# A four-layer graph network on one core: layer 2's aggregation by single graphs, with an earlier form of the setup

## The chip, the cores and the metric

The kernel runs on one core of a Trainium2 chip. The time is the device time of one execution in microseconds, the median of several runs. The engines are named as in the profile: PE (TensorE, matmuls), PEld (its weight loads), DVE (VectorE), ACT (ScalarE), POOL (GpSimd) and SP (which issues most of the DMA transfers).

## What is computed

There are 128 graphs of 64 nodes with 256 features each, and one adjacency matrix for all. Four layers follow each other, each as `x = layernorm(x + layer(x))`.

```python
# layer 0: attention over the adjacency matrix
Wh = h @ W;  e = leaky_relu(Wh@a1[:, None] + Wh@a2[None, :]);  e = where(adj == 0, -inf, e)
h_prime = softmax(e) @ Wh
# layer 1: attention over a list of 512 edges (src, dst), 4 heads
Xq, Xv = H @ W_lin.T, H @ W_val.T
e = (leaky_relu(Xq[:, src] + Xq[:, dst]) * a).sum(-1) + log(adj[src, dst] + eps)
Y = segment_sum(segment_softmax(e, src) * Xv[:, dst], src) @ W_out.T
# layer 2: normalised aggregation and two batch-normed products
A_norm = adj + eye;  dinv = rsqrt(deg);  A_hat = A_norm * dinv[:, None] * dinv[None, :]
agg = einsum('nm,bmd->bnd', A_hat, x)
out = batchnorm(relu(batchnorm(agg @ W1.T + b1)) @ W2.T + b2)
# layer 3: two graph products, then LSTMs over windows of 1 to 4 nodes
```

The change concerns the line `agg`, and the work done once at the start: weights and indices are loaded, the edges are sorted by source, and matrices are built that gather by matmul.

## The kernel before

A block `q` is 8 graphs, 512 tokens, as 4 chunks of 128 tokens (two graphs each); there are 16 blocks. Layers 0, 1 and the first product of layer 2 are interleaved in one main loop: while block `q` goes through the edges of layer 1 (`l1_graph`), block `q+2` goes through layer 0, and block `q-3` through the end of layer 1 and the aggregation.

```python
# the aggregation, L402 to L408: aht is A_hat twice, on the diagonal of a 128x128 matrix
def v_c(q):
    x2 = L1.pop(q)["x2"]
    for k in range(KD):
        p_ = bank([PQ, P])
        for c in range(PQ):
            nc.tensor.matmul(p_[:, c, :], x2[:, c, k * P:(k + 1) * P], aht, start=True, stop=True)
        nc.scalar.activation(A[:, q, k * QT:(k + 1) * QT], p_.rearrange("p c t -> p (c t)"), AF.Copy)
```

The product of attention and values in layer 1 (L381) already goes by single graphs, in tiles of 64 rows and 64 columns:

```python
for c in range(PQ):
    for h in range(HEADS):
        for s in range(2):
            r = slice(s * N, (s + 1) * N)
            r0 = (h % 2) * 64
            nc.tensor.matmul(pY[s][r0:r0 + 64, h // 2, c, :], v[r, c, h * 64:(h + 1) * 64],
                             am[r, c * HEADS + h, :], start=True, stop=True)
```

The setup. Its scratch tiles lie in A, the big array that holds the blocks' results later (`su.tile`):

```python
load_x(0)
nc.scalar.dma_start(w0[:, :, :D], i["L0_gnn_W"]...)
nc.scalar.dma_start(aL0, i["L0_gnn_a"].partition_broadcast(P))
nc.sync.dma_start(row_i, i["L1_gnn_src"].partition_broadcast(P))
# ... the columns of indices, the adjacency matrix, load_x(1)
nc.scalar.dma_start(wq[:, :, :D], i["W_linT"]...)
# ... aL1, acol, wv

def own(q, shape, name):     # block 0 of layer 0 has its tiles in A, the others in the pool
    return work.tile(shape, F32, name=name, bufs=1) if q else su.tile(shape, F32, name)

perm = [work.tile([P, E], F32R, name="hi", bufs=4) for c in range(EC)]

def setup_l0():              # L415, L416: two more columns for w0
    ...
        nc.vector.tensor_mul(tmp, w0[:, :, :D], aL0[:, None, n * D:(n + 1) * D].to_broadcast([P, KD, D]))
        nc.vector.reduce_sum(w0[:, :, D + n], tmp, axis=AX.X)

def setup_ends():            # L466: the sorted edges by matmul with the permutation
    for n in range(2):
        pe_ = bank([E])
        for c in range(EC):
            nc.tensor.matmul(pe_, wide[n][:, c, :], perm[c], start=c == 0, stop=c == EC - 1)
        nc.vector.tensor_copy(ends[:, n, :], pe_)
    # ... and 16 matmuls of two columns (L471)

l0_a(0); setup_l0(); ...; l0_b(0); setup_order(); l0_c(0); l0_a(1); setup_ends()
l0_b(1); l0_d(0); setup_gather(); setup_queries(); l0_e(0); l0_c(1); setup_signs()
l0_d(1); l1_t(0); l1_qv(0, 0); l0_e(1); l1_qv(0, 1)
# (each on a line of its own in the kernel)
wout = weights(wa, "wout", i["W_outT"]); w1 = ...; w2 = ...
setup = [setup_zero, setup_segments, setup_bias, setup_pairs]
setup += [lambda c=c: setup_count(c) for c in range(EC)]
setup += [setup_place, setup_adjacency]      # one of these after each step of the main loop
```

The main loop, and in it the edge products and their split in two parts (L316, L319, L320):

```python
nc.tensor.matmul(z, L1[q]["qs"][c][:, s, k * P:(k + 1) * P], gath_r, start=True, stop=True)
nc.scalar.activation(hi, z, AF.Relu)
nc.vector.scalar_tensor_tensor(lo, z, 0.0, hi.bitcast(F32), op0=OP.max, op1=OP.subtract)
```

Of the kernel before, what the change touches and what calls it, by code (L numbers as in the profile page):

```python
# [40 lines left out]
def kernel(ctx: ExitStack, tc: tile.TileContext, i, out):  # L41
# [59 lines left out]
    nc.vector.memset(bd, 0.0)  # L101
    bdT = const.tile([P, P], F32, name="bdT")
# [8 lines left out]
    with ExitStack() as two:  # L111
# [17 lines left out]
        class su:  # L129

            free = NQ * 2 * QT

            @classmethod
            def tile(cls, shape, dtype, name):
                size = 1
                for n in shape[1:]:
                    size *= n
                cls.free -= size
                t = A.rearrange("p q c -> p (q c)")[:shape[0], cls.free:cls.free + size]
                t = t if dtype == F32 else t.bitcast(dtype)  # L140
                if len(shape) == 3:
                    t = t.rearrange("p (a b) -> p a b", b=shape[2])
                elif len(shape) == 4:
                    t = t.rearrange("p (a b c) -> p a b c", b=shape[2], c=shape[3])
                return t


        load_x(0)
        w0 = wa.tile([P, KD, D + 2], F32, name="w0")
        nc.scalar.dma_start(w0[:, :, :D], i["L0_gnn_W"].rearrange("(k p) c -> p k c", p=P))  # L150
        aL0 = su.tile([P, 2 * D], F32, name="aL0")
        nc.scalar.dma_start(aL0, i["L0_gnn_a"].partition_broadcast(P))
        col_i = su.tile([P, EC, 2], I32, name="col_i")
        row_i = su.tile([P, E], I32, name="row_i")
        nc.sync.dma_start(row_i, i["L1_gnn_src"].partition_broadcast(P))
        for n, e in enumerate(("L1_gnn_src", "L1_gnn_dst")):
            nc.sync.dma_start(col_i[:, :, n], i[e].rearrange("(c p) -> p c", p=P))
        for s in range(2):
            nc.sync.dma_start(bd[s * N:(s + 1) * N, s * N:(s + 1) * N], i["adj"])
# [5 lines left out]
        aL1 = su.tile([P, D], F32, name="aL1")  # L165
        nc.scalar.dma_start(aL1, i["L1_gnn_a"].rearrange("h d -> (h d)").partition_broadcast(P))
        acol = su.tile([P, KD], F32, name="acol")
        nc.sync.dma_start(acol, i["L1_gnn_a"].rearrange("h d -> (h d)").rearrange("(c p) -> p c", p=P))
        nc.sync.dma_start(wv, i["W_valT"].rearrange("(k p) c -> p k c", p=P))
# [16 lines left out]
        def own(q, shape, name):  # L186

            return work.tile(shape, F32, name=name, bufs=1) if q else su.tile(shape, F32, name)

        def transposed(src, q=1):  # L190

            t = own(q, [P, KD, QT], "tT")
            for k in range(KD):
                p_ = bank([PQ, P])
                for c in range(PQ):
                    nc.tensor.transpose(p_[:, c, :], src[:, c, k * P:(k + 1) * P], ident)  # L196
                nc.scalar.activation(t[:, k, :], p_.rearrange("p c t -> p (c t)"), AF.Copy)
            return t
# [8 lines left out]
        def l0_a(q):  # L207
            L0[q] = {"x": xin.pop(q)}
            L0[q]["xT"] = transposed(L0[q]["x"], q)

        def l0_b(q):
            xT = L0[q]["xT"]
            wh = L0[q]["wh"] = own(q, [P, PQ, D + 2], "wh")
# [7 lines left out]
            sb = L0[q]["sb"] = own(q, [P, PQ, P], "sb")  # L221
            nc.gpsimd.tensor_copy(sb, wh[:, :, D + 1:].to_broadcast([P, PQ, P]))

        def l0_c(q):
# [4 lines left out]
            t = own(q, [P, PQ, P], "lr")  # L229
# [14 lines left out]
        def l0_d(q):  # L244
            e = L0[q]["e"]
            p_ = bank([PQ, P])
            for c in range(PQ):
                nc.tensor.transpose(p_[:, c, :], e[:, c, :], ident)
            eT = L0[q]["eT"] = own(q, [P, PQ, P], "eT")
            nc.scalar.activation(eT, p_, AF.Copy)  # L250
# [151 lines left out]
        def v_c(q):  # L402
            x2 = L1.pop(q)["x2"]
            for k in range(KD):
                p_ = bank([PQ, P])
                for c in range(PQ):
                    nc.tensor.matmul(p_[:, c, :], x2[:, c, k * P:(k + 1) * P], aht, start=True, stop=True)  # L407
                nc.scalar.activation(A[:, q, k * QT:(k + 1) * QT], p_.rearrange("p c t -> p (c t)"), AF.Copy)  # L408


        def setup_l0():

            tmp = su.tile([P, KD, D], F32, name="tmp")
            for n in range(2):
                nc.vector.tensor_mul(tmp, w0[:, :, :D], aL0[:, None, n * D:(n + 1) * D].to_broadcast([P, KD, D]))  # L415
                nc.vector.reduce_sum(w0[:, :, D + n], tmp, axis=AX.X)  # L416


        iota_e = su.tile([P, E], F32, name="iota_e")
# [6 lines left out]
        for s in range(2):  # L426
            nc.gpsimd.iota(node[s * N:(s + 1) * N, :], pattern=[[0, 1]], base=0, channel_multiplier=1,
                           allow_small_or_imprecise_dtypes=True)
        for n in range(2):
            nc.gpsimd.memset(spads[n], 0.0)  # L430
        ends = su.tile([P, 2, E], F32, name="ends")
        cols = su.tile([P, EC, 2], F32, name="cols")
        ohT = su.tile([P, 2, E], F32, name="ohT")
        ones = su.tile([P, P], F32, name="ones")
        nc.gpsimd.memset(ones, 1.0)
        eps8 = su.tile([P, 1], F32, name="eps8")
        nc.gpsimd.memset(eps8, 1e-8)
        again = su.free

        perm = [work.tile([P, E], F32R, name="hi", bufs=4) for c in range(EC)]  # L440
        wide = [work.tile([P, EC, P], F32R, name="lo", bufs=4) for n in range(2)]
        col_r = work.tile([P, EC, 2], F32R, name="lo", bufs=4)

        def setup_order():
            col_f = su.tile([P, EC, 2], F32, name="col_f")
            nc.vector.tensor_copy(col_f, col_i)
            nc.vector.tensor_copy(col_r, col_f)
            key_r = su.tile([P, E], F32, name="key_r")
            key_c = su.tile([P, EC], F32, name="key_c")
            nc.vector.tensor_copy(key_r, row_i)  # L450
            nc.vector.scalar_tensor_tensor(key_r, key_r, float(E), iota_e, op0=OP.mult, op1=OP.add)
            nc.vector.scalar_tensor_tensor(key_c, col_f[:, :, 0], float(E), iota_c, op0=OP.mult, op1=OP.add)
            for n in range(2):
                nc.gpsimd.tensor_copy(wide[n], col_f[:, :, n:n + 1].to_broadcast([P, EC, P]))
            rank = su.tile([P, EC], F32, name="rank")
            less = su.tile([P, E], F32, name="less")
            for c in range(EC):
                nc.vector.tensor_scalar(less, key_r, key_c[:, c:c + 1], 0.0, op0=OP.is_lt, op1=OP.add,
                                        accum_out=rank[:, c:c + 1])
                nc.vector.tensor_scalar(perm[c], iota_e, rank[:, c:c + 1], None, op0=OP.is_equal)  # L460

        def setup_ends():
            for n in range(2):
                pe_ = bank([E])
                for c in range(EC):
                    nc.tensor.matmul(pe_, wide[n][:, c, :], perm[c], start=c == 0, stop=c == EC - 1)  # L466
                nc.vector.tensor_copy(ends[:, n, :], pe_)
            pcol = bank([EC, 2])
            for r in range(EC):
                for c in range(EC):  # L470
                    nc.tensor.matmul(pcol[:, r, :], perm[c][:, r * P:(r + 1) * P], col_r[:, c, :],  # L471
                                     start=c == 0, stop=c == EC - 1)
            nc.vector.tensor_copy(cols, pcol)

        def setup_gather():

            nc.vector.tensor_scalar(ohT, ends, node, None, op0=OP.is_equal)
            nc.vector.tensor_add(gath_r, ohT[:, 0, :], ohT[:, 1, :])

        def setup_queries():  # L480

            tmp = su.tile([P, KD, D], F32, name="tmp2")
            nc.vector.tensor_mul(tmp, wq[:, :, :D], aL1[:, None, :].to_broadcast([P, KD, D]))
            for k in range(KD):
                nc.vector.reduce_sum(wq[:, k, D:], tmp[:, k, :].rearrange("p (h d) -> p h d", h=HEADS), axis=AX.X)
            nc.vector.scalar_tensor_tensor(aL1, aL1, -1.0, aL1, op0=OP.mult, op1=OP.max)
            nc.vector.tensor_scalar_mul(aL1, aL1, 1.0 - SLOPE)
            nc.vector.tensor_mul(wq[:, :, :D], wq[:, :, :D], aL1[:, None, :].to_broadcast([P, KD, D]))

        def setup_signs():  # L490
            below = su.tile([P, KD], F32, name="below")
            nc.vector.tensor_scalar(below, acol, 0.0, None, op0=OP.is_lt)
            nc.vector.scalar_tensor_tensor(acol, acol, 0.0, below, op0=OP.is_gt, op1=OP.subtract)
# [20 lines left out]
        l0_d(1)  # L514
        l1_t(0)
        l1_qv(0, 0)
        l0_e(1)
        l1_qv(0, 1)


# [465 lines left out]
```

## Time and profile before

| what | us |
|---|---|
| time, median of 3 (2338.16 to 2341.32) | 2340.56 |
| span of the profiled execution | 2338.7 |
| PE busy | 2227.4 |
| DVE busy | 1016.9 |
| ACT busy | 911.3 |
| aggregation, L407, 256 instructions, PE busy | 34.2 |
| edge products, L316, 256 instructions, PE busy | 110.6 |
| LSTM products, L873 and L879, PE busy | 801.4 and 435.9 |

A row of a group names line, engine and operation, then output and inputs, the shape, the number of instructions, the busy time and the mean of one in ns, and last the idle time before them with what ended it. A row of the timeline has the start and duration in us, then the same. In the chain, start and duration stand before the engine and line. A row with several instructions covers the time from the first's start to the last's end. The main loop runs until about 700 us; from there the rest of layer 2 and layer 3 follow, which the change does not touch.

### The profile page before, as it was taken

The numbers are of one execution on the slowest core, as the hardware profiler recorded it, in microseconds if no ns is written. First come the engines' busy times: TensorE is split into PE (matmuls) and PEld (weight loads), VectorE is DVE, ScalarE is ACT, GpSimd is POOL, SyncE is SP. The second block draws the span as 40 slices with busy tenths as digits, with TensorE's granted clock in tenths as the row PEclk, the third lists the DMA queues.
The fourth block names the chain that finished last, engine by engine and source line by source line (L and its number), as shares of the span: only waits on it lengthen the run. The fifth ranks groups of instructions, "written<-read, shape, count | busy, mean of one in ns | idle before, by whom it ended". The sixth has DMA issues, their size and how long they took to land.

```text
span 2338.7 us, 25909 instructions
## 1 busy us (share of the span) xinstructions
PE 2227.4 (95%) x9649; PEld 1536.6 (66%) x9649; DVE 1016.9 (43%) x2317; ACT 911.3 (39%) x1885; POOL 412.5 (18%) x536
## 2 busy tenths in 40 slices
PE   6989999999999997999999999999999999999996
PEld 5767777777654445577578578568568568568475
DVE  7666776777744444232332332332332422422322
ACT  3755565556434701333233233233333333333331
POOL 2123233233220002011211211110210210210101
PEclk8999999999999998999999999999999999999998
DMA  3022023202224002000100100100100100100100
GB/s 116 19 39 48 29 47 57 39 30 37 39 39 108 18 0 96 3 19 8 47 19 1 54 19 1 55 19 1 54 19 1 54 19 1 46 9 1 36 0 28
DMA packets 126654, 74.50 MB, mean 32 GB/s; under 512 B 81856, under 2 KB 117312, under 8 KB 126272
## 3 DMA queue, kind: packets, MB, share of 16 engines
q1 hardware_dynamic: 124672, 70.87, 12.3%
q8 instruction: 76, 1.25, 0.2%
q0 software_dynamic: 1024, 1.05, 0.2%
q10 hardware_dynamic: 832, 0.92, 0.1%
q14 instruction: 50, 0.41, 0.1%
HBM read 44.25 MB, written 28.57 MB: 31 GB/s over the span
## 4 chain that ended last, share of the span: by engine, by line
PE 87%; DVE 6%; ACT 3%; POOL 1%; DMA 1%; issue 1%; SPq 0%; POOLq 0%; DVEq 0%; ACTq 0%
PE l L873 32%; PE l L879 18%; PE g L827 5%; PE pz L735 5%; PE pz L671 5%; PE e L307 3%; PE g L835 2%; PE m L282 2%; PE m L217 2%; PE m L395 2%; PE z L316 2%; PE m L285 2%; PE m L407 1%; PE m L196 1%; PE m L381 1%
## 5 line engine op out<-in xcount | busy, mean ns | idle before, releaser
L873 PE MATMUL l<-H,wih 128*128 128x256 f32 (+2 forms) x2496 | 801.4, 472 | 0.4 <-DVE H L844 0.2
L873 PEld LDWEIGHTS l<-H,wih 128*128 128x128 f32 x2496 | 467.2, 191 | 246.5 <-issue 158.8
L879 PE MATMUL l<-hid,whh 128*128 128x256 f32 (+2 forms) x1536 | 435.9, 437 | 0.0
L879 PEld LDWEIGHTS l<-hid,whh 128*128 128x128 f32 x1536 | 291.8, 190 | 128.4 <-issue 61.2
L885 ACT ACTIVATE gate_i<-l,bias 128x256 f32<-128x256 f32 (+2 forms) x176 | 100.3, 570 | 646.1 <-PE l L879 514.7
L888 DVE TENSOR_TENSOR gate_i<-gate_i,gate_g 128x256 f32<-128x256 f32 (+2 forms) x96 | 47.8, 498 | 571.2 <-ACT gate_g L885 571.2
L889 POOL TENSOR_TENSOR cell<-gate_f,cell 128x256 f32<-128x256 f32 (+2 forms) x96 | 83.7, 872 | 1018.5 <-ACT gate_f L885 1018.5
L320 DVE SCALAR_TENSOR_TENSOR lo<-z,hi 128x512 fp32r<-128x512 f32 x256 | 167.5, 680 | 61.5 <-ACT hi L319 60.2
L319 ACT ACTIVATE hi<-z 128x512 fp32r<-128x512 f32 x256 | 143.9, 597 | 105.6 <-PE z L316 104.4
L82 POOL TENSOR_TENSOR ln_rs<-ln_rs,mhalf 128x2 f32<-128x2 f32 (+1 forms) x96 | 86.8, 904 | 516.2 <-DVE ln_ng L94 516.1
L885 ACT ACTIVATE gate_g<-l,bias 128x256 f32<-128x256 f32 (+2 forms) x176 | 100.2, 569 | 107.8 <-PE l L873 59.0
L885 ACT ACTIVATE gate_o<-l,bias 128x256 f32<-128x256 f32 (+2 forms) x176 | 99.5, 566 | 71.4 <-PE l L879 54.0
L307 PE MATMUL e<-lo,apad 128*128 128x512 f32 x256 | 110.7, 432 | 14.1 <-DVE lo L320 14.0
L827 PE MATMUL g<-wg,hT 128*128 128x256 f32 x512 | 123.6, 387 | 0.0
L316 PE MATMUL z<-gath_r,qs 128*128 128x512 f32 x256 | 110.6, 482 | 8.2 <-DVE lo L320 8.2
L892 DVE TENSOR_TENSOR cell<-gate_i,gate_g 128x512 f32<-128x512 f32 (+2 forms) x80 | 48.3, 604 | 154.7 <-ACT gate_g L885 154.6
L827 PEld LDWEIGHTS g<-wg,hT 128*128 128x128 f32 x512 | 99.1, 195 | 24.0 <-issue 10.5
L671 PE MATMUL pz<-A,w 128*128 128x512 f32 x256 | 112.5, 595 | 0.0
L307 PE MATMUL e<-hi,apad 128*128 128x512 f32 x256 | 108.5, 424 | 2.2 <-ACT hi L319 2.0
L893 ACT ACTIVATE gate_g<-cell 128x256 f32<-128x256 f32 (+2 forms) x176 | 89.9, 511 | 51.8 <-DVE cell L892 36.8
L898 DVE TENSOR_TENSOR H<-gate_o,gate_g 128x512 f32<-128x512 f32 (+2 forms) x80 | 47.6, 595 | 105.7 <-PE l L873 89.8
L671 PEld LDWEIGHTS pz<-A,w 128*128 128x128 f32 x256 | 48.2, 191 | 56.0 <-issue 54.6
(210 smaller groups left out, 2783.0 us busy)
## 6 DMA issues: line engine op xcount, KB each, us to landing
xin<-in_x SPq DMA_DIRECT2D x16, 512.0 KB
ld<-table SPq DMA_DIRECT2D x16, 512.0 KB
x_dram<-x SPq DMA_DIRECT2D x16, 512.0 KB
x2r<-x_dram SPq DMA_DIRECT2D x32, 256.0 KB
x_dram<-A SPq DMA_DIRECT2D x64, 128.0 KB
x3r<-x_dram SPq DMA_DIRECT2D x64, 128.0 KB
out<-st SPq DMA_DIRECT2D x64, 128.0 KB
wih<-in_WihT SPq DMA_DIRECT2D x3, 1024.0 KB
```

Of the source, the lines that this page charges most:

```text
L82: nc.gpsimd.tensor_tensor(dst, dst, mhalf[:, :n], OP.pow)
L307: nc.tensor.matmul(pes[S], apad[:, k, P - HEADS - r0:2 * P - HEADS - r0], t, start=first and n == 0, stop=False)
L316: nc.tensor.matmul(z, L1[q]["qs"][c][:, s, k * P:(k + 1) * P], gath_r, start=True, stop=True)
L319: nc.scalar.activation(hi, z, AF.Relu)
L320: nc.vector.scalar_tensor_tensor(lo, z, 0.0, hi.bitcast(F32), op0=OP.max, op1=OP.subtract)
L671: nc.tensor.matmul(p_, w1[:, k, m * P:(m + 1) * P], A[:, q, k * QT:(k + 1) * QT], start=k == 0, stop=k == KD - 1)
L735: nc.tensor.matmul(p_, w2[:, k, m * P:(m + 1) * P], hidden(q, k), start=k == 0, stop=k == M1 - 1)
L827: nc.tensor.matmul(p_[:, c, :], hT[:, k, c * P:(c + 1) * P], wg[n][:, k, :], start=k == 0, stop=k == KD - 1)
L873: nc.tensor.matmul(gates[n], wih[p][:, k, mw * P:(mw + 1) * P], Hw[:, k, :, s, :], start=k == 0, stop=not s and k == KD - 1)
L879: nc.tensor.matmul(gates[n], whh[p][:, k, m * P:(m + 1) * P], hid[:, k], start=False, stop=k == KD - 1)
L885: nc.scalar.activation(act[n], gates[n], AF.Tanh if n == "g" else AF.Sigmoid, bias=bias[:, p - 1, m:m + 1])
L893: nc.scalar.activation(act["g"], cell[:, j], AF.Tanh)
```

## The change

The aggregation multiplies each graph by its own 64 rows and columns of `aht`, instead of a chunk of two graphs by the 128x128 matrix, half of which is zeros. The upper graph uses the upper half of TensorE's rows and the lower one the lower half, and each writes to a bank of its own, so that the two halves may work at the same time. The setup is the one from before it was restructured: all loads in source order with the weights ahead, both blocks of layer 0 in the same pool of tiles and one after the other, and then all steps for layers 1 and 2 in one row ahead of the main loop; nothing of it is left to be done in the loop.

```diff
+    for s in range(2):
+        nc.sync.dma_start(bd[s * N:(s + 1) * N, s * N:(s + 1) * N], i["adj"])
...
         load_x(0)
+
         w0 = wa.tile([P, KD, D + 2], F32, name="w0")
-        nc.scalar.dma_start(w0[:, :, :D], i["L0_gnn_W"].rearrange("(k p) c -> p k c", p=P))
-        aL0 = su.tile([P, 2 * D], F32, name="aL0")
-        nc.scalar.dma_start(aL0, i["L0_gnn_a"].partition_broadcast(P))
...
+        nc.sync.dma_start(w0[:, :, :D], i["L0_gnn_W"].rearrange("(k p) c -> p k c", p=P))
         load_x(1)
...
         nc.scalar.dma_start(wq[:, :, :D], i["W_linT"].rearrange("(k p) c -> p k c", p=P))
...
+        nc.scalar.dma_start(wv, i["W_valT"].rearrange("(k p) c -> p k c", p=P))
+        wout = weights(wa, "wout", i["W_outT"], nc.scalar)
+        w1 = weights(wa, "w1", i["W1T"], nc.scalar)
+        w2 = weights(wa, "w2", i["W2T"], nc.scalar)
...
-            wh = L0[q]["wh"] = own(q, [P, PQ, D + 2], "wh")
+            wh = L0[q]["wh"] = work.tile([P, PQ, D + 2], F32, name="wh", bufs=1)
...
         def v_c(q):
             x2 = L1.pop(q)["x2"]
+
+            p_ = [bank([KD, PQ, N]) for _ in range(2)]
             for k in range(KD):
-                p_ = bank([PQ, P])
                 for c in range(PQ):
-                    nc.tensor.matmul(p_[:, c, :], x2[:, c, k * P:(k + 1) * P], aht, start=True, stop=True)
-                nc.scalar.activation(A[:, q, k * QT:(k + 1) * QT], p_.rearrange("p c t -> p (c t)"), AF.Copy)
+                    for s in range(2):
+                        r = slice(s * N, (s + 1) * N)
+                        nc.tensor.matmul(p_[s][:, k, c, :], x2[r, c, k * P:(k + 1) * P], aht[r, r],
+                                         start=True, stop=True)
+            dst = A[:, q, :].rearrange("p (k c s t) -> p s k c t", k=KD, c=PQ, s=2)
+            for s in range(2):
+                nc.scalar.activation(dst[:, s], p_[s], AF.Copy)
...
+        aL0 = bcast(su, "aL0", i["L0_gnn_a"])
...
+        for n in range(2):
+            for step in (l0_a, l0_b, l0_c, l0_d, l0_e):
+                step(n)
...
+        zero = su.tile([P, 36, SROWS], F32, name="zero")
+        nc.vector.memset(zero, 0.0)
...
+        perm = su.tile([P, EC, E], F32, name="perm")
...
+        wide = su.tile([P, EC, 2, P], F32, name="wide")
+        nc.vector.tensor_copy(wide, col_f[:, :, :, None].to_broadcast([P, EC, 2, P]))
...
+                nc.tensor.matmul(pe_, wide[:, c, n, :], perm[:, c, :], start=c == 0, stop=c == EC - 1)
...
+        l1_t(0)
+        l1_qv(0, 0)
+        l1_qv(0, 1)
...
-                if setup:
-                    setup.pop(0)()
```

## The prediction

> **What bounds the kernel now.** I read the page first: busy time, then the chain that ended last, then the groups. After that came a table by stretches and the timeline.
>
> ```profile
> PE 2227.4 (95%) x9649; PEld 1536.6 (66%) x9649; DVE 1016.9 (43%) x2317; ACT 911.3 (39%) x1885; POOL 412.5 (18%) x536
> ...
> PE 87%; DVE 6%; ACT 3%; POOL 1%; DMA 1%; issue 1%; SPq 0%; POOLq 0%; DVEq 0%; ACTq 0%
> ```
>
> TensorE bounds the whole: 87% of the chain is its work. The change touches only two places, so I asked what ends last in each. The stretches show that the setup is another stage altogether (columns: stretch, its length, then busy time of PE, PEld, DVE, ACT and POOL, the granted clock, DMA share, GB/s):
>
> ```profile
> 0.00:7.20 7.20, 1.51 (x7) 1.55 (x8) 0.71 (x3) 1.67 (x2) 2.08 (x14) 1.00 0.75 219
> 7.20:58.00 50.80, 35.62 (x143) 27.57 (x142) 43.63 (x135) 15.75 (x48) 10.53 (x12) 0.87 0.33 102
> 58.00:100.00 42.00, 39.10 (x187) 30.00 (x186) 26.96 (x64) 29.99 (x71) 6.63 (x12) 1.00 0.08 26
> ```
>
> From 7.2 to 58 us VectorE is busy for 43.6 of 50.8 us, 86%; TensorE waits for it. Before 7.2 us nobody computes much: VectorE waits for a load. From 58 us on, TensorE leads again (39.1 of 42 us). The ends of the setup in the timeline:
>
> ```profile
> 7.21 0.69 DVE L415 TENSOR_TENSOR A<-w,A 128x512 f32<-128x512 f32 x1 [5.64 <-DMA A<-in_L_gnn_a]
> ...
> 18.98 1.19 PE L466 MATMUL m<-hi,lo 128*128 128x512 f32 x4 [0.25 <-ACT tT L197]
> ...
> 55.60 0.66 DVE L320 SCALAR_TENSOR_TENSOR lo<-z,hi 128x512 fp32r<-128x512 f32 x1
> ...
> 56.98 1.04 PE L316 MATMUL z<-gath_r,qs 128*128 128x512 f32 x3
> ```
>
> The first row says that VectorE sat idle 5.64 us for the vector of layer 0; the last two that the steady edge loop of layer 1 (L316, L320) begins at about 57 us. One more row matters: `seg`'s memset, written in the source behind the first steps of the main loop, ran at 1.08 us. So instructions are placed on an engine by when their inputs should be ready, not strictly by source order, and I assume the same for the changed kernel.
>
> The second place is layer 2's aggregation, in the groups and in the chain:
>
> ```profile
> L407 PE MATMUL m<-aht,x 128*128 128x128 f32 x256 | 34.2, 286 | 4.4 <-POOL x L96 2.8 <-ACT v L295 1.5
> ...
> L381 PE MATMUL m<-am,v 64*64 64x64 f32 x1024 | 26.0, 223 | 2.7 <-issue 1.2 <-POOL am L374 1.1
> ```
>
> ```profile
> 257.36 1.82 PE m L407 x16
> 302.89 2.02 PE m L407 x16
> ```
>
> Each of the 16 blocks runs 8 matmuls as 16 instructions (every fp32 matmul is two here), some 1.9 us, 32 to 34 us in all, and these stand on the chain: what is saved here shortens the end.
>
> **What the Trainium skill says.** "TensorEngine Tiling (Array Packing)", section "Theoretical Speedup", gives up to 2x where a dimension is 64 or less, and its section "Key Properties" says that tiles can load weights and multiply in parallel. The trace agrees for 64x64 tiles: L381's 64 pairs of load and multiply at 165.02 us were through when L217's load began at 166.11, 17 ns per pair. "TensorE: Matmul & The Clock Gate", section "LDWEIGHTS (loading the stationary operand)", says that a load's time goes with its columns and not with its rows: "A 32×128 weight load takes the same time as a 128×128 weight load". The trace agrees in the columns: a load of 128 columns (L407) has a median of 192 ns, one of 64 (L381) 135 ns, 57 ns for 64 columns. Nothing before shows 64 rows with 128 columns. On the loads, "DMA: Bandwidth & Descriptors", section "Issuing engines are not separate DMA queues", says that transfers issued by different engines run on the same 16 DMA engines and interleave. Here the early loads from the two queues together keep those engines 0.75 busy.
>
> **The aggregation.** The two 64x64 blocks of `aht` are multiplied apart: 16 matmuls instead of 8, with 64 rows and 64 moving columns each, alternating between upper and lower half: 32 instructions for 16. Streaming halves. In the trace a pass of 256 columns takes 217 ns (four of L285 in 0.87 us), so 128 columns take 108 ns and 64 take 54 ns. But the stationary operand stays x2 with 128 columns. From the 57 ns above, such a load takes about 114 ns. Now a pair takes 1.94/16 = 121 ns (L407's first load at 256.97, the next line's at 258.91), about the longer of 108 and 114. Three outcomes per block:
> - both halves in parallel, each bound by its 16 loads: 16 x 114 to 121 = 1.8 to 1.9 us, 0.1 us less; in 16 blocks -1.6 us. I give this 0.65.
> - loads hidden, bound by streaming: 16 x 61 = 1.0 us, 0.9 us less; less a little for the evacuation, -13 us. 0.25.
> - the halves load one after the other: 32 x 114 = 3.6 us, or partly so; I take +20 us. 0.10.
> Weighted: -1.0 - 3.3 + 2.0 = -2.3 us. ScalarE's two evacuations of 128x512 (599 ns) stay, but neither can start before all the matmuls are done, as both banks are filled to the last pair. ScalarE has room (29.99 of 42 us), so I add nothing.
>
> **The setup.** The old order comes back. Its terms:
> - *Loads.* The vector of layer 0 now stands behind x of two blocks, w0 and all five other weight matrices: 0.5+0.25+0.5 MB on its own queue and 0.25 x 3 + 0.5 x 2 MB on the other, with its own 0.25 some 3 MB. In the trace of before the first 12.25 us moved 2.8 MB (sum of its GB/s slices over 1.75 us). So it lands at about 12.2 instead of 7.2 us: +5.0 us before VectorE starts.
> - *VectorE's work.* Of the 43.6 us, about 3.2 are main loop (six of L293 at 0.42, one L320); 2.4 us of setup ran after 58 us (L575, L595, L598 and the small ones). So the setup is 42.8 us. New is the widening copy that GpSimd did: 1024 elements, about 0.8 us (L477, as wide, took 0.755). The 2304-element memset (some 2.2 us from seg's 0.486 for 513) has no inputs and fits into the idle start. With the 3.2 us of first queries again: 46.8 us at 86% is 54.4 us, from 12.2 to 66.6, where it was 58. So +8.6 us with the loads.
> - *TensorE.* The permutation is plain fp32 now: 8 matmuls of 512 columns become 16 instructions at 0.44 us (L671: 112.5/256), 7.0 us for 2.4, and the 16 tiny ones become 32, +1.8 us. VectorE still has layer 0's and the query weights' work then, so most is hidden: +1.
> - *Two blocks of layer 0* now share their single buffers, so block 1's products wait until block 0's are read. VectorE fills the gap with the rest: +1, with a tail.
> - *Moved out of the main loop:* the bias and adjacency matmuls (1.07+1.12+1.0 us), which TensorE did in its own time in the first blocks, two table loads of 1.28 us on ScalarE, and a 1.6 us TensorE wait behind them at 75.4 us: -4.
> Sum of the setup: 8.6+1+1-4 = +6.6 us.
>
> Together +6.6 - 2.3 = +4.3 us, 2345 us; since the setup's uncertain terms lean upward I say 2346.
>
> **The rivals.** *The setup falls apart*: if VectorE follows the source order more than I assume, the steps of layer 1 wait for both blocks of layer 0 (about 18 us each in a row after the loads), and the loop starts at 80 to 90 us: 2360 to 2375. For it speaks that layer 0 alone has long waits in the trace (ScalarE 11.5 us for the row maxima); against it the early memset. *The aggregation wins*: the halves overlap like L381's, -13 to -15 us, and the setup costs 6: 2332. For it speaks the 17 ns per pair; against it that those tiles load only 64 columns. *The later loads are hidden*: the first transposes need only x (5.68 us), and if the vector of layer 0 comes through early, the setup costs 2 us: 2340. *Serial halves*: TensorE pays 1.3 us or more per block: 2365.
>
> **Range and chances.** 2% is 47 us. No term or sum of likely terms reaches it: the aggregation's whole cost is 34 us, and the setup would have to double. The range joins the second rival below (2330) and the first above (2370).
>
> **What will show it.** VectorE's first L0 product at about 12 us instead of 7.2. The first steady edge matmuls at 64 to 70 us instead of 57. The aggregation's 32 instructions: 1.8 to 2.0 us per block if loads bind, about 1.0 if not. I am wrong if the aggregation falls to 1 us or goes over 2.5, if the loop starts past 80 us, or if the first 100 us after the setup lose or gain more than 4 us.

## The result: 39 us slower

The changed kernel takes 2378.5 us (2377.72 to 2379.75), the kernel before 2339.4 us beside it; the ratio is 1.017, 95% interval 1.0152 to 1.0187. The prediction was 2346 us with 2330 to 2370 us as its range. The page of the changed kernel, busy time and chain:

```profile
PE 2253.8 (95%) x9929; PEld 1552.5 (65%) x9929; DVE 1019.5 (43%) x2320; ACT 912.8 (38%) x1885; POOL 407.9 (17%) x531
...
PE 87%; DVE 6%; ACT 3%; POOL 2%; DMA 2%; issue 1%; SPq 0%; POOLq 0%; ACTq 0%; DVEq 0%
```

TensorE is busy for 26 us more, but the shares hardly move: these lines say nothing of where the time went. The landmarks in the trace do. Each is the start of a weight load in us; the last row is the span.

| landmark | before | changed | new aggregation alone | old setup alone |
|---|---|---|---|---|
| first aggregation | 181.4 | 199.1 | 176.5 | 199.9 |
| last edge product of layer 1 | 624.0 | 655.6 | 632.8 | 642.4 |
| last product of layer 2 | 876.7 | 911.0 | 888.2 | 895.3 |
| first LSTM product | 925.5 | 964.1 | 937.5 | 948.1 |
| span | 2338.7 | 2377.9 | 2350.6 | 2361.3 |

Before to changed, the stretches between these rows add 17.7, 13.9, 2.7, 4.3 and 0.6 us, 39.2 in all. The last two columns are the first two experiments. The setup costs at the start and once more ahead of layer 3; the aggregation costs in the main loop. Such landmarks are good to some 4 us at the start: run 13, which differs from the kernel before in layer 3 alone, runs the same products in the same order and reaches the first aggregation at 177.3 instead of 181.4 us. From 50 to 60 us its granted clock was 1.00, and 0.83 in the trace of the kernel before. So the setup costs 18 to 22 us at the start, and the 176.5 of the third column is no gain.

**The start.** The same stretches as in the prediction (length, busy time of PE, PEld, DVE, ACT and POOL, granted clock, DMA share, GB/s), of the changed kernel:

```profile
0.00:7.20 7.20, 1.67 (x8) 1.57 (x8) 3.11 (x7) 1.37 (x2) 1.82 (x12) 1.00 0.76 233
7.20:58.00 50.80, 30.08 (x90) 19.63 (x88) 28.11 (x84) 10.95 (x31) 8.14 (x12) 0.87 0.33 105
58.00:100.00 42.00, 37.29 (x166) 28.01 (x164) 28.92 (x78) 20.86 (x55) 1.17 (x3) 0.84 0.05 13
```

VectorE is busy for 28.1 of 50.8 us where it had been busy for 43.6: it isn't overloaded, it waits. Rows of the timeline of the changed kernel:

```profile
12.72 0.69 DVE L408 TENSOR_TENSOR A<-w,A 128x512 f32<-128x512 f32 x1 [4.98 <-DMA A<-in_L_gnn_a]
...
20.58 0.43 DVE L460 CAST A<-A 128x512 f32<-128x512 int32 x1 [1.42 <-DMA A<-in_L_gnn_src]
...
42.01 1.13 DVE L201 SCALAR_TENSOR_TENSOR lr<-m,wh,mask 128x128 f32<-128x128 f32 x4 [4.70 <-PE m L198]
...
51.05 7.54 PE L476 MATMUL m<-A 128*128 128x512 f32 x16
...
62.09 0.17 DVE L484 COPY A<-m 128x8 f32<-128x8 f32 x1 [2.77 <-PE m L481]
...
83.69 0.71 PE L286 MATMUL z<-gath_r,qs 128*128 128x512 f32 x2
```

The permutation was finished on VectorE at 33.2 us, but the matmuls that use it (L476) start at 51.05, behind all of block 1 of layer 0. Nothing that needs the sorted edges can run on VectorE until then, and of other work it has only block 1's: 4.7 us idle for block 1's transposes, 2.8 us for L481. The steady edge products begin at 83.7 us, where they had begun at 57.

**The aggregation.** Its group, and one block of it in the timeline:

```profile
L380 PE MATMUL m<-aht,x 64*128 64x64 f32 x512 | 40.9, 283 | 4.7 <-POOL x L96 2.9 <-ACT v L265 1.3
```

```profile
277.88 0.52 PEld L380 LDWEIGHTS m<-aht,x 64*128 64x128 f32 x4 [0.36 <-issue]
277.88 2.72 PE L380 MATMUL m<-aht,x 64*128 64x64 f32 x32
278.39 0.17 ACT L264 ACTIVATE spad<-m 64x4 f32<-64x4 f32 x1
278.61 1.86 PEld L380 LDWEIGHTS m<-aht,x 64*128 64x128 f32 x28 [0.21 <-ACT spad L264]
```

The same of a block in the kernel before:

```profile
256.73 0.19 PEld L307 LDWEIGHTS e<-lo,apad 128*128 128x128 f32 x1
256.97 2.02 PEld L407 LDWEIGHTS m<-aht,x 128*128 128x128 f32 x16
```

The busy time went from 34.2 to 40.9 us. Four loads of one half run, 110 ns apart, and then TensorE stands until ScalarE has emptied another tile at 278.56; only then do both halves go. The block takes 2.65 us from its first load to the next line's, where the old one took 1.78 or 1.94. It also starts later: the old block's first load comes 0.24 us after the load ahead of it (256.73 to 256.97), the new one's 0.56 us after it, 0.36 of them idle, and no wait is shown for them.

### The profile page after: what moved, and what is told of

The parts are those of the page before. It is cut to its first block, busy times and chain, and to the rows that moved or that the text cites. A ratio compares the mean times of both kernels' runs of the same rounds, so it can differ in the third digit from the quotient of the medians.

```text
span 2377.9 us, 26465 instructions
## 1 busy us (share of the span) xinstructions
PE 2253.8 (95%) x9929; PEld 1552.5 (65%) x9929; DVE 1019.5 (43%) x2320; ACT 912.8 (38%) x1885; POOL 407.9 (17%) x531
## 4 chain that ended last, share of the span: by engine, by line
PE 87%; DVE 6%; ACT 3%; POOL 2%; DMA 2%; issue 1%; SPq 0%; POOLq 0%; ACTq 0%; DVEq 0%
PE l L824 32%; PE l L830 18%; PE pz L622 5%; PE g L778 5%; PE pz L686 5%; PE e L277 4%; PE g L786 2%; PE m L252 2%; PE m L365 2%; PE m L187 2%; PE z L286 2%; PE m L255 2%; PE m L380 2%; PE m L228 1%; PE m L166 1%
## 5 line engine op out<-in xcount | busy, mean ns | idle before, releaser
L840 POOL TENSOR_TENSOR cell<-gate_f,cell 128x256 f32<-128x256 f32 (+2 forms) x96 | 83.7, 872 | 1018.5 <-ACT gate_f L836 1018.5
L622 PEld LDWEIGHTS pz<-A,w 128*128 128x128 f32 x256 | 48.6, 193 | 57.3 <-issue 55.2
```

The source lines that it names most:

```text
L622: nc.tensor.matmul(p_, w1[:, k, m * P:(m + 1) * P], A[:, q, k * QT:(k + 1) * QT], start=k == 0, stop=k == KD - 1)
```

## The experiments

The runs were timed in groups, each beside the kernel before, which took 2336.3 to 2339.4 us in them. The ratio is to that time; where a repair is said to save so many us, it is the change in the excess over it, 39.1 us for the changed kernel.

**1 and 2: each half of the change alone.** The kernel before with the new `v_c`; the changed kernel with the old one.

> The kernel before, with the new aggregation alone. Theory A (the aggregation itself costs: 32 pairs at 60 to 64 ns plus the wait for two banks at once): its instructions are busy about 41 us instead of 34.2, and the time is 2339 + 6 to 7 = 2345 to 2346 us. Rival B (the aggregation is neutral, as the load-bound case of the prediction had it, and all 39 us come from the setup): 2337 to 2340 us.

> The changed kernel with the old aggregation of 128 rows. Theory A: 2378.5 - 6 to 7 = 2371 to 2373 us, the loop's first edge product still at about 78 us. Rival B: 2378 to 2380 us.

Measured: aggregation alone 2352.3 us (ratio 1.0069, 1.005 to 1.0087), setup alone 2362.1 us (1.0101, 1.008 to 1.0122), beside 2337.0 us of the kernel before. So +15 and +25 us, which together make the 39 us (40.3). The aggregation is not neutral, and costs twice what its busy time suggested: rival B falls, and A was right in kind only. In the trace of the aggregation alone, its 16 blocks take 42.8 us from first load to the next line's, before 35.0. By block:

| block | before | new aggregation alone |
|---|---|---|
| ten of the main loop, alternating | 1.78, 1.94 us | 2.35, 2.66 us |
| the same, from the load ahead of the block | 2.55, 2.18 us | 3.12, 3.21 us |
| the last three, in layer 2 | 2.10 us | 1.93 us |
| the same, from the load ahead of the block | 2.53 us | 2.88 us |

In the loop the new form loses 0.57 or 0.72 us within the block, and nothing in the last three. That pointed at the banks. It isn't all: in the last three the old form's first load runs while the product ahead of it still does, and counts into its 2.10 us; the new form's waits longer, and with this start it is slower there too, by 0.35 us. In every second block of the loop the start is 0.32 us later as well. From the load ahead, the 16 blocks take 55.2 us instead of 44.2, 11.1 more.

**3: other banks for the sorted edges.** Layer 0 and the setup share three general banks, which go round in the order of the source. In this run only the edges' matmuls get banks that stand empty then:

```diff
-            pe_ = bank([E])
+            pe_ = bank([E], name="z", bufs=3)
...
-        pcol = bank([EC, 2])
+        pcol = bank([EC, 2], name="e", bufs=2)
```

> The changed kernel, only that the sorted edges (16 + 32 instructions) are written to PSUM banks that the setup doesn't use otherwise, in place of the three banks that go round among layer 0's steps. Theory C (these matmuls stand behind block 1 of layer 0 because their banks come round only after it): they start at 33 to 40 us instead of 51, VectorE fills its idle time from 37 to 55 us with the pair counts, the first edge product comes 10 to 14 us earlier than 77.8 us, the time is 2364 to 2369 us. Rival D (VectorE's amount of work and the late loads set the start): the matmuls move but the first edge product by less than 5 us, 2374 to 2379 us.

Measured: 2371.8 us (1.0144, 1.0124 to 1.0164), 4 us less. Two rows of its timeline, the first of the edges' matmuls and the transposes of block 0 for layer 1:

```profile
29.94 2.08 PE L476 MATMUL z<-A 128*128 128x512 f32 x2
64.48 1.91 PE L166 MATMUL m<-ident,A 128*128 128x128 f32 x8
```

The matmuls start at 29.94 instead of 51.05 us, as C says and more, but the first edge product of all comes at 71.2 instead of 77.8 us, 6.6 us earlier, between the two theories. The transposes now stood behind the adjacency's matmuls, until 64.5 us; run 7 tests whether for the same reason.

**4: the aggregation in tiles of 64 rows and 64 columns**, in the kernel before: 32 matmuls of 64 stationary columns, written to the upper and lower half of the same two banks.

```diff
+                    for j in range(2):
                         for s in range(2):
                             r = slice(s * N, (s + 1) * N)
-                            nc.tensor.matmul(p_[s][:, k, c, :], x2[r, c, k * P:(k + 1) * P], aht[r, r],
+                            o = slice(j * N, (j + 1) * N)
+                            nc.tensor.matmul(p_[s][o, k, c, :], x2[r, c, k * P + j * N:k * P + (j + 1) * N], aht[r, r],
                                              start=True, stop=True)
```

> The kernel before, with the aggregation in tiles of 64 rows and 64 columns: 32 matmuls, 64 instructions. Theory E (the changed aggregation is bound by loads of 128 columns, 120 to 128 ns in each half): loads of 64 columns in four tiles give 17 to 27 ns per pair, 1.1 to 1.7 us per block in place of 1.94, and with the waits for both banks 2328 to 2337 us. Rival (the halves hinder each other, or the waits cost more than the loads save): 2339 to 2348 us, as with the new aggregation or worse.

Measured: 2339.1 us, ratio 1.0005 (0.9993 to 1.0018): no difference to the kernel before, and within the rival's range. The blocks fall to 1.09 us in the last three, but take 1.50 and 1.81 us in the loop; from the load ahead these are 2.27 and 2.37 us, where the kernel before has 2.55 and 2.18. Small tiles save the loads, the wait for the banks and the later start stay.

**5: the weights' place.** Ahead of layer 3 the changed kernel loses 4.3 us. The chain of the kernel before, and then of the changed one, where layer 3 begins (start, duration, what):

```profile
877.76 0.37 SPq L76
878.18 5.16 DMA x2r<-x_dram
883.44 0.70 DVE x2r L809
```

```profile
912.03 0.37 SPq L76
912.45 0.47 SPq L76
913.22 0.37 SPq L76
913.64 9.28 DMA x2r<-x_dram
923.01 0.70 DVE x2r L760
```

L76 is a weight load of 1 MB for the LSTMs. Before, one is issued just ahead of layer 3's first x; now three are, because the second of four waits for the last use of a weight tile of layer 2 whose place in memory it takes, and the queue keeps its order. The run puts the three tiles `wout`, `w1`, `w2` last in their pool again, with the same loads.

> The changed kernel; the three weight tiles of layers 1 and 2 are placed last in their pool, as before, and not ahead of the masks. Theory F (the place of w2 decides how many 1 MB weight loads of layer 3 wait for its last use and then stand ahead of layer 3's first x): the gap between the last product of layer 2 and the first of the LSTM falls from 53 to 49 us, the time by 4 us to 2374 to 2375 us. Rival (the gap follows from the shifted start of the loop): no change, 2377 to 2380 us.

Measured: 2373.4 us (1.0152, 1.0134 to 1.0169), 4 us less; the LSTM's gap is 49.2 us instead of 53.1, as theory F has it. In the chain one load is left and x lands in 5.34 us:

```profile
910.46 0.37 SPq L76
910.88 5.34 DMA x2r<-x_dram
916.32 0.70 DVE x2r L760
```

**6: the loads of before**, by need: layer 0's weights and vector first on one queue, the indices behind x on the other, the large weights last.

> The changed kernel with the loads of before (by need, in the same queues), the rest of its setup as changed. Theory G (late loads cost what they delay VectorE's first product, 12.7 instead of 7.2 us): the first edge product 5 to 6 us earlier than 77.8 us, time 2371 to 2374 us. Rival (VectorE is idle later anyway, the loads are hidden): first edge product less than 2 us earlier, 2376 to 2379 us.

Measured: 2372.2 us (1.0146, 1.0129 to 1.0163), 5 us less. VectorE's first product is at 7.08 us, 5.6 us earlier; the first edge product comes at 74.0 us, 3.8 earlier and not the 5 to 6 of theory G. The edges' matmuls stay behind block 1, at 46.8 us.

**7: other banks for all matmuls of the setup**, as in run 3, with those of bias and adjacency too.

> The changed kernel with all matmuls of the setup (edges, bias, adjacency) in PSUM banks that layers 0 and 1 don't use at that time. The run with the edges alone brought the first edge product from 77.8 to 71.2 us; then the transposes of block 0 stood behind the adjacency's matmuls, whose banks come round ahead of them. Theory C: they no longer do, the first edge product comes at 62 to 67 us, time 2362 to 2368 us. Rival D (VectorE's counts set the start): not before 70 us, 2370 to 2373 us.

Measured: 2368.8 us (1.0129, 1.0112 to 1.0146), 9 us less; the first edge product at 66.5 us. That is in C's range, the time just over it, and both are out of D's. The transposes of block 0 now run at 60.5 us, ahead of the adjacency's last matmuls (65.9), so it was the same reason. The edges' matmuls start at 30.45 us, but end only at 51 us, cut into pieces between layer 0's steps; that the late loads are the reason is shown by the next two runs.

**8 and 9: the three repairs together, and without the weights' place.**

> The three edits in one: loads by need, all setup matmuls in other banks, weight tiles last. If they add up: the first edge product at 57 to 61 us and the LSTM's gap 49 us, time 2378 - 4 - 5 - 12 = 2355 to 2360 us; what then remains over the kernel before is the aggregation (12 to 15 us) and little else. If a further cause in the setup is missing (the plain fp32 permutation, block 1 behind block 0): 2362 us or more.

> The changed kernel with loads by need and all setup matmuls in other banks, the weight tiles placed as changed. Theory I (loads and banks each hide a part of the other): the first aggregation starts at 177 to 179 us, against 199.1 changed, 195.1 with the loads alone and 190.9 with the banks alone; the LSTM's gap stays at 53 us; time 2354 to 2356 us. Rival (the place of the weights acts in the setup too): first aggregation at 184 to 188 us, 2360 to 2365 us.

Measured: all three 2350.9 us (1.0053, 1.0036 to 1.007); loads and banks alone 2352.7 us (1.0072, 1.0055 to 1.0089). That is 12.4 and 16.5 us over the kernel before, where the new aggregation in the setup of before has 15.3: the setup's cost is found. What these runs keep of the old setup (block 1 behind block 0, the plain fp32 permutation, nothing left to the loop) costs nothing more that these times show. The sum of single gains was 4 + 5 + 9 = 18 us, together it is 27, more than was expected. The ninth run says where the rest is: loads and banks together bring the first aggregation from 199.1 to 176.0 us, 23 us, where they had brought 4.0 and 8.2 us singly. Each hides a part of the other. With the order of the banks as changed, early indices leave the edges' matmuls at 46.8 us, and with late indices (20.6 us) free banks let them end at 51. With both, in the run of all three repairs, the edges are sorted before block 0 has left layer 0:

```profile
16.88 2.07 PE L478 MATMUL z<-A 128*128 128x512 f32 x4
19.22 4.83 PE L478 MATMUL z<-A 128*128 128x512 f32 x10
24.56 1.02 PE L478 MATMUL z<-A 128*128 128x512 f32 x2
25.64 3.74 PE L483 MATMUL e<-A 128*128 128x2 f32 x32
```

The gap ahead of the LSTM is 49.4 us with the weights' place and 52.9 without, as in run 5, and the excesses differ by 4.1 us.

**10 to 12: four general banks.** PSUM's eight banks are cut as 3 general + 3 for edge products + 2 for edge scores. A control cuts 4 + 3 + 1 in the kernel before (and 4 + 4 instead of 5 + 3 in layer 2); then the same with the new aggregation, and with that of run 4.

```diff
-        def bank(shape, name="m", bufs=3):
+        def bank(shape, name="m", bufs=4):
...
-                pes[S] = bank([E], name="e", bufs=2)
+                pes[S] = bank([E], name="e", bufs=1)
```

> A control: the kernel before with the PSUM banks cut otherwise, four instead of three for the general tiles and one instead of two for the edge scores. Its own effect is not known: one bank less for the scores makes every second block wait for the softmax's first read, one more for the rest saves waits. 2335 to 2350 us.

> The kernel before with the new aggregation and the same cut of the banks as the control. Theory H (of the 12 to 15 us that the new aggregation costs, most is the wait for its second bank, 0.4 to 0.7 us in each block of the loop): with four general banks its blocks take about 1.95 us as in the last three blocks, and the time is within 3 us of the control. Rival (the 32 pairs in place of 16 cost by themselves): 10 to 15 us over the control.

> As the run before, with the tiles of 64 rows and 64 columns. Theory H with E: without the wait a block takes 1.1 to 1.3 us instead of 1.8 to 1.94, 8 to 12 us under the control. Rival: the same time as with the other two aggregations.

Measured beside 2339.0 us of the kernel before: control 2329.3 us (0.9963, 0.9949 to 0.9977), new aggregation 2330.3 us (0.9962, 0.9948 to 0.9976), tiles of 64x64 2326.0 us (0.9942, 0.9925 to 0.9958). The control lies below its range. Theory H holds: with a free bank the new aggregation costs 1 us instead of 15. One block of it and one of the small tiles, in these two runs:

```profile
251.27 1.86 PEld L410 LDWEIGHTS m<-aht,x 64*128 64x128 f32 x32 [0.36 <-issue]
251.27 2.00 PE L410 MATMUL m<-aht,x 64*128 64x64 f32 x32
```

```profile
251.61 1.02 PEld L412 LDWEIGHTS m<-aht,x 64*64 64x64 f32 x64 [0.36 <-issue]
251.61 1.16 PE L412 MATMUL m<-aht,x 64*64 64x64 f32 x64
```

All 32 loads run without a break, 54 ns apart (111 within a half), 1.93 us to the next line's; the old form takes 1.91 us in the control, and the small tiles 1.09 us. The later start stays in both: their first load comes 0.54 to 0.56 us after the load ahead of it, that of the old form 0.23 to 0.24. With it the 16 blocks take 42.3 us in the control, 46.8 with the new aggregation and 31.7 with the small tiles. Of the 10.6 us less the medians show 3.3 with overlapping intervals, not the 8 to 12 expected: most of the saving is lost to other waits, which weren't sought out.

**13: x of layer 3 first**, in the kernel before: its first two transfers are put ahead of the last LSTM weights.

> The kernel before; the first two transfers of x for layer 3 are put ahead of the loads of the last LSTM weights. Theory F (what stands ahead in the queue sets when layer 3 starts): x is there when layer 2 ends, the gap from the last product of layer 2 to the first of the LSTM falls from 49 to 43 or 44 us, the time to 2332 to 2334 us. Rival (the weights are needed soon after, and the gap only moves): 2336 to 2340 us.

Measured: 2337.9 us, ratio 1.0 (0.9992 to 1.0009), in the rival's range. The wait for x is gone from the chain, and the gap is 49.0 us as before. In its chain another path stands in the place, by statistics, scale and transposes:

```profile
875.21 0.51 DVE bn_mv L652
875.97 0.55 POOL sc L82
877.19 0.61 ACT st L800
877.84 0.92 PE g L805 x3
878.78 0.70 DVE x2r L806
```

The addition of x comes 6.7 us after the last product's load (872.1), as in the kernel before (876.7 to 883.44). There the transfer ended just when this path did, and was hidden; in the changed kernel, with 9.28 us, it was not (12.0 us).

**14: the repaired setup, small tiles and four banks in one.**

> The repaired setup of the three edits, the aggregation in tiles of 64 rows and 64 columns, and four general PSUM banks. If the parts add up: the repaired setup brought the first aggregation 4 us earlier than before, so 2326 - 4 = 2320 to 2324 us. Rival (the cut of the banks and the setup's use of the loop's banks collide, or the setup's order shifts): 2326 to 2332 us.

Measured: 2325.2 us (0.9958, 0.9942 to 0.9975), beside 2336.3 us: no further gain over the small tiles with the setup of before, 2326.0 us (0.9942). Both beat both kernels. The expectation took the repaired setup to be 4 us ahead of the setup of before (177.4 against 181.4 us to the first aggregation); but run 13 reaches it at 177.3 with the setup of before, so there was nothing to add.

## Why the prediction was wrong

*The loads.* Right for the vector of layer 0: predicted at 12.2 us, its product ran at 12.72. But I followed only this one transfer. The indices came late too, 20.58 instead of 8.54 us, and the repaired order needed the early loads (runs 7 to 9, which move vector and indices together). That the 12.2 came so near is partly luck: the named transfers with its own make 3.25 MB, not 3, and at the rate taken from the kernel before (2.8 MB in 12.25 us) they land after 14 us. But the changed kernel moved 280 GB/s in its first 12 us, the kernel before 228.

*"46.8 us at 86%."* This is the step that failed most. I took the 86% from the kernel before, as if it belonged to VectorE. It belonged to an order of steps that kept VectorE supplied; in the changed kernel it is 28.1 of 50.8 us, 55%, and the steady edge products came at 83.7 us, not at 64 to 70. I had seen that a memset was moved up and took all steps to be as movable. The memset needs no PSUM bank. A step that needs one of three banks in turn keeps its place among all users of these banks, whatever its inputs: run 3, which changed nothing but the banks, moved the edges' matmuls from 51 to 30 us. The first rival, "the setup falls apart", named the right outcome (80 to 90 us; 83.7 measured), with the source order as its reason and the memset as the argument against it. Two of the signs of being wrong came: the loop starts past 80 us, and blocks of the aggregation take over 2.5 us (2.65).

*TensorE's permutation, "most is hidden: +1".* The size was right (7.5 us for 16 instructions, predicted 7.0), the place wrong: from 51 to 62 us it is on the path. *Block 1, "+1, with a tail"*: it held up the edges by its whole length, through the banks. *Moved out of the loop, -4*: no run measures it by itself, but run 8 compared with the new aggregation in the setup of before has the first edge product at 58.0 instead of 47.9 us and the first aggregation at 177.4 instead of 176.5: the loop's first blocks regain 9 of the 10 us. The setup as a whole, predicted +6.6, measured +25: in the trace of the setup alone 18.5 us up to the first aggregation and 4.0 us ahead of layer 3, which the prediction hadn't at all.

*The aggregation's instructions.* The case I gave 0.65 came true: both halves in parallel, each bound by 16 loads of 128 columns. Predicted 1.8 to 1.9 us, measured 1.93 where no bank is waited for. The Trainium skill, "TensorE: Matmul & The Clock Gate", section "LDWEIGHTS (loading the stationary operand)", had said that rows don't count; this case shows it now, as a half's pair of 64 rows takes 111 ns (run 11), as one of 128 rows does (1.78/16). The factor of up to 2 in "TensorEngine Tiling (Array Packing)", section "Theoretical Speedup", isn't there for 64 rows with 128 columns; with 64 columns it is 1.75 (1.91 to 1.09 us). "Nothing before shows 64 rows with 128 columns" was a misreading: the setup of the kernel before has two such loads, which start 109 ns apart.

```profile
68.93 0.29 PEld L577 LDWEIGHTS m<-A 64*128 64x128 f32 x2 [0.36 <-DVE e L234]
```

They showed the missing term as well: the later start (0.55 us after the load ahead) stands in no sum of the prediction.

*"I add nothing" for the evacuation.* I looked at ScalarE's room and at the end of the block. The cost is at its start: two banks must be free at once, where the old form took one and then the next. It measured 0.57 to 0.72 us in ten blocks of the loop, -2.3 us in the prediction became +15. Of these 15 us the blocks themselves hold 7.8, and with their later start 11.1. With a fourth bank in both forms 4.5 of the 11.1 are left (46.8 against 42.3 us), all of it in the start. That the change from 128 to 64 rows causes the later start is not isolated, but it comes in all twelve blocks of the loop in runs 11 and 12 and in none of the control. What makes up the rest of the 15 us stays open.

## What to carry to other kernels

An engine's share of busy time in one schedule says nothing of another: ask for each step which buffer it takes its turn for, and follow the banks as you follow the data. Matmuls split into row halves save streaming, not weight loads, and as written here want two banks at once; split the columns as well, and give them a free bank, or leave it. Count a block from the instruction ahead of it, or a late start is missed. Two late things can hide each other, so repair them together before you call one harmless.

## What the runs showed that was not expected

- Four general PSUM banks and one for the scores, a mere control, gain 0.37% (0.23 to 0.51): the last edge product comes at 610.1 us, where run 13, with the main loop of before, has it at 619.2.
- Where a weight tile lies in memory cost 4 us some 900 us later: a 1 MB load that waits for that place holds up the loads behind it, and layer 3's x lands in 9.28 instead of 5.16 us.
- With four general banks a block of 64-row tiles starts 0.32 us later than one of 128 rows, after 0.36 us in which no load runs and no wait is shown. That is much of the 0.8 us that the small tiles save within a block.
- Removing a 5 us transfer from the chain of the kernel before changed nothing, as another path ended at the same time: the chain shows one of two.
